# Group-norm statistics of batch entries 1 to 3 taken beside blocks of the first layer, and two steps of key preparation in a slot while an attention waits

## The chip, the cores and the metric

The kernel runs on one core of one Trainium2 chip. The metric is the device time of one execution in microseconds (us). Of a kernel several executions are timed and the median is taken; in addition one execution is recorded by the hardware profiler, and all durations below come from that one. Engines are named as in the profile: PE is the matrix engine (PEld its weight loads), DVE the vector engine, ACT the engine for activation functions, POOL the general one, and SP the engine from whose queue the transfers (DMAs) are issued.

## The reference, cut to what matters

The input `x` has 4 batch entries of 32 x 96 tokens (3072 tokens) with 256 channels, all in float32. Two layers are computed, each adding to `x`.

```python
def _gn(v, G=32, eps=1e-5):              # group norm: mean and variance per entry and
    g = v.reshape(B_, H_, W_, G, C_ // G)  # group of 8 channels, over all 3072 tokens
    m = jnp.mean(g, axis=(1, 2, 4), keepdims=True)
    s = jnp.var(g, axis=(1, 2, 4), keepdims=True)
    return ((g - m) / jnp.sqrt(s + eps)).reshape(v.shape)

# layer 0: a Mamba block along one image axis ("t"), then another along the other ("d")
x = x + _L0_conv_ref(_gn(x), ...)
# layer 1: additive attention within an entry, then a graph-gated mixture of 4 experts
t = _to_tokens(x)
t = t + _L1_attn_ref(_ln_t(t), ...)      # h = tanh(q_i + k_j + b); e = h . wa; softmax over j
t = t + _L1_ffn_ref(_ln_t(t), ...)
```

A Mamba block projects in, convolves over 4 steps, computes a decay and an input for each of 512 channels x 16 states, scans along time, sums over the states, gates and projects out. The attention needs a tanh for every pair of tokens and 32 hidden units: 4 x 3072 x 3072 x 32 of them. The group norm needs the statistics of the whole entry before the first token of that entry can be normalized. Each attention needs the keys and queries of all 3072 tokens of its entry, and these need the finished first layer of that entry.

## The kernel before, in words

**First layer.** `Layer0.run` (L551) walks through 64 blocks of 384 tokens. In the listing order they are: for entry 0 the eight "t" blocks, then block 0 of the "t" blocks of entry 1, then the eight "d" blocks of entry 0; for entry 1 the remaining seven "t" blocks, the first "t" block of entry 2, the eight "d" blocks of entry 1; and so on. So blocks 0 to 16 end entry 0, blocks 17 to 32 end entry 1, 33 to 48 entry 2, 49 to 63 entry 3. Blocks 0 to 16 are called `lead`: no attention runs beside them, and some of their work is put on other engines (sums over states by PE, some element-wise work on ACT) than in the later blocks. Block *n* is worked through in 48 slots; in them its scans and outputs (`back`, L353) are done, together with the projection and convolution of block *n + 1* (`front`, L172) and the last sums of block *n - 1* (`end`, L508). Each slot has two halves: the functions of `jobs[0]` (the scans, L402, and the decays dA on ACT, L385), then everything else (the inputs dB, L393, the front, the end). dB and the scans use tiles `bB` and `bC` that are loaded two ahead on the SP queue, 384 KB each. A block has 32 dB instructions, two in every three slots. They serve below as a clock of the slots.

**The order of work.** PE, ACT, DVE and POOL get their instructions in exactly the order in which these Python functions are called; only the DMA issues on SP are ordered by a scheduler. DVE, ACT and POOL work through their lists in that order, so an instruction that has to wait holds up everything behind it on its engine.

**Group norm before.** `group_norm` (L99) runs once, ahead of everything, for all four entries: for each entry and each half *k* of the channels it loads two pieces of 768 KB (two buffers of the tag "dt"), takes six `bn_stats` of 512 tokens (L120) and one aggregate; then a small matmul averages over the groups of 8 channels, three small DVE operations and a second matmul give the variance, and ACT takes the square root (L131). One reciprocal for all entries ends it (L132).

**Attention.** `whole` (L1949) steps the first layer alone until block 17 has reached slot 11, where entry 0 is known to be stored; then `Attention.units` (L778) and the first layer advance together, half a slot of each in turn. With one tanh of 128 x 3072 per slot (L815), an entry takes 768 slots. The scores of a tanh are computed two slots later by 16 small matmuls (L788), and after every eighth tanh there are softmax and value steps. Work that is less urgent (`side`: key preparation, and `after`, which prepares the second half of layer 1) is advanced by `beside()`, one step at a time, in slots where the attention has nothing else to do.

**Keys.** `keys(b)` (L720) yields 48 steps. The first 12 take layer-norm statistics of 256 tokens each (tile `x`, 256 KB, two buffers, L690; `bn_stats` L707 and aggregate L708). Then 12 times three steps follow: normalize two tiles (L703); transpose them on PE (L717) and copy the result out of PSUM (`xTc`, L718); multiply with both weights on PE (`pq`, L748) and copy into `qsel` (four small copies, L752) and `krep` (L755). Transposes and products share one PSUM buffer. Only when the 48 steps are done can the first tanh of that entry be issued. While `units` finds no `krep` for the next entry, it takes the branch at L803: no tanh, and one `beside()` per slot:

```python
            if b < B and "krep" not in self.state[b]:
                yield                      # first half of a slot of layer 0
                ...                        # late copies
                yield                      # second half
                beside()
                continue
```

**The end.** After block 63 no first layer is left; the rest of the attention runs beside a sort of the graph's edges (DVE), gathers (POOL) and early experts (PE, `early`). Then follows a tail with gathers, gates and the remaining experts.

Of the kernel before, what the change touches and what calls it, by code (L numbers as in the profile page):

```python
# [17 lines left out]
F32 = mybir.dt.float32  # L18
# [8 lines left out]
P = 128  # L27
B, NV, S, C = 4, 32, 96, 256
TOK = NV * S
# [45 lines left out]
class Layer0:  # L75
# [8 lines left out]
    def __init__(self, ctx, tc, ident, a, x1):  # L84
        self.nc = nc = tc.nc
        self.ident, self.a, self.x1 = ident, a, x1
        pool = lambda name, bufs, **k: ctx.enter_context(tc.tile_pool(name=name, bufs=bufs, **k))
        self.const, self.wk, self.st = pool("l0c", 1), pool("l0w", 1), pool("l0s", 2)
        self.ps, self.ps_u = pool("l0p", 1, space=PSUM), pool("l0u", 1, space=PSUM)
        self.dram = pool("l0d", 1, space=bass.MemoryType.DRAM)  # L90
        self.ps_x = pool("l0x", 1, space=PSUM)
        ps_a = pool("l0a", 1, space=PSUM)
        self.dA = [ps_a.tile([P, 512], F32, tag=f"dA{i}", name=f"dA{i}") for i in range(DA_BUFS)]
        self.turn, self.beside = 0, None
        self.xt = [self.dram.tile([KC, P, NV, S], F32, tag="xt", name="xt", bufs=3)
                   for _ in range(B)]
        self.group_norm()

    def group_norm(self):  # L99

        nc, wk, ps, const = self.nc, self.wk, self.ps, self.const
        gavg = const.tile([P, P], F32, tag="gavg", name="gavg")
        nc.sync.dma_start(gavg, self.a["gavg"])
        eps = const.tile([P, 1], F32, tag="eps", name="eps")
        nc.vector.memset(eps, 1e-5)
        self.gm = const.tile([P, KC, B], F32, tag="gm", name="gm")
        self.gr = const.tile([P, KC, B], F32, tag="gr", name="gr")
        HB = TOK // 2
        NB = HB // 512
        for b in range(B):  # L110
            gm = self.gm[:, :, b]
            mv = wk.tile([P, KC, 2], F32, tag="gmv", name="gmv")
            gv = wk.tile([P, KC], F32, tag="gv", name="gv")
            for k in range(KC):
                stats = wk.tile([P, 2, NB, 6], F32, tag="gst", name="gst")
                for i in range(2):
                    xs = wk.tile([P, HB], F32, tag="dt", name="xs", bufs=2)
                    nc.sync.dma_start(xs, self.a["xT"][k * P:(k + 1) * P, b, i * HB:(i + 1) * HB])
                    for j in range(NB):
                        nc.vector.bn_stats(stats[:, i, j, :], xs[:, j * 512:(j + 1) * 512])  # L120
                nc.vector.bn_aggr(mv[:, k, :], stats.rearrange("p i n s -> p (i n s)"))
            pg = ps.tile([P, T], F32, tag="pp", name="pg")
            nc.tensor.matmul(pg[:, :KC], gavg, mv[:, :, 0], start=True, stop=True)
            nc.vector.tensor_copy(gm, pg[:, :KC])

            nc.vector.tensor_tensor(gv, mv[:, :, 0], gm, ALU.subtract)
            nc.vector.tensor_tensor(gv, gv, gv, ALU.mult)
            nc.vector.tensor_tensor(gv, gv, mv[:, :, 1], ALU.add)
            pg2 = ps.tile([P, T], F32, tag="pp", name="pg2")
            nc.tensor.matmul(pg2[:, :KC], gavg, gv, start=True, stop=True)  # L130
            nc.scalar.activation(self.gr[:, :, b], pg2[:, :KC], AF.Sqrt, bias=eps)  # L131
        nc.vector.reciprocal(self.gr, self.gr)  # L132

    def weights(self, way, keys, bufs=1):

# [416 lines left out]
    def run(self):  # L552

        order, NBLK = [], TOK // T
        for b in range(B):
            order += [(b, "t", i) for i in range(1 if b else 0, NBLK)]
            if b + 1 < B:
                order.append((b + 1, "t", 0))  # L560
            order += [(b, "d", i) for i in range(NBLK)]
        blocks = [{"b": b, "way": w, "i": i, "L": S if w == "t" else NV, "lead": n <= 2 * NBLK}
                  for n, (b, w, i) in enumerate(order)]

        FRONT, STATES = ("in_x", "conv", "convb", "xproj", "dt", "dtb"), ("A", "D", "in_z")

        def states_weights(blk):
            blk["w"] = {**self.weights(blk["way"], ("A", "D"), 2), **self.weights(blk["way"], ("in_z",))}
            self.scale_states(blk["w"])

        first = blocks[0]
        self.wf = self.weights(first["way"], FRONT)
        self.scale_front(self.wf)
        states_weights(first)

        def alone(*parts):
            for slot in range(48):
                fs = [f for part in parts for f in part.get(slot, [])]
                for f in fs:
                    f()  # L580
                if fs:
                    yield None
                    yield None

        yield from alone(self.front(first, True))
        left, ending = ({}, {}), {}
        for n, blk in enumerate(blocks):
            then = blocks[n + 1] if n + 1 < len(blocks) else None
            old = blocks[n - 1] if n else None

            fresh = then and n + 2 < len(blocks) and blocks[n + 2]["way"] != then["way"]
            if old is None or old["way"] != blk["way"]:
                for t in self.dA:
                    self.nc.vector.memset(
                        t[:, :T].rearrange("p (q l) -> p q l", l=blk["L"])[:, :, 0:1], 0.0)
            for j in range(2):
                for name in ("bB", "bC"):
                    if not left[1]:
                        self.broadcast(blk, name, j)

            breaks = then and (then["way"], then["i"]) == ("d", 0) and then["b"] == blk["b"]
            jobs, later = self.back(blk, None if breaks else then)
            ahead = self.front(then, blk["lead"]) if then and not breaks else {}
            for slot in range(48):
                for f in left[0].get(slot, []) + jobs[0].get(slot, []):
                    f()
                yield None
                for part in (left[1], jobs[1], ending, ahead):
                    for f in part.get(slot, []):
                        f()  # L610
                if slot == 12:
                    if old is None or old["way"] != blk["way"]:
                        blk["wo"] = self.weights(blk["way"], ("out",))
# [24 lines left out]


class Attention:  # L640
# [135 lines left out]
    def units(self, side):  # L776
# [24 lines left out]
        while i < B * PER + LAG or todo or self.later:  # L801
            b, col = self.entry, self.col = divmod(i, PER)
            if b < B and "krep" not in self.state[b]:  # L803

                yield
                late, self.later = self.later, []
                for f in late:
                    f()
                yield
                beside()  # L810
                continue
# [433 lines left out]
class Graph:  # L1245
# [864 lines left out]
```

## Time and profile before

| What | us |
|---|---|
| Median of three executions (lowest, highest) | 15310.87 (15308.61, 15326.58) |
| The profiled execution, its own time | 15328.57 |
| Its span, first to last instruction | 15326.8 |
| PE, DVE, ACT, POOL busy in it | 11744.9, 11006.6, 12153.9, 8997.6 |

The span and the time of the profiled execution differ by 1.8 us, so sums over the span stand directly for time; that execution lies 17.7 us above the median. A row of instruction groups gives source line, engine, operation, output<-input with shapes and count; then the total busy time and the mean duration in ns; then the engine's idle time just before them and what ended it. "Granted clock" is the share of full speed that PE was given. A row of a table of stretches gives, behind the stretch and its length, the busy time and number of instructions of each engine, then the granted clock, the mean busy share of the 16 DMA engines and their GB/s.

### The profile page before, as it was taken

To read this page: it belongs to the slowest core of one execution; us is meant where nothing else is said; L and a number is where in the kernel's file an instruction comes from. 1 tells how busy PE (TensorE), PEld (TensorE's weight loads), DVE (VectorE), ACT (ScalarE), POOL (GpSimd) and SP (SyncE) were. 2 spreads that over 40 slices of the span, in tenths; PEclk is the share of its full clock that TensorE was granted. 3 is DMA by queue.
4 is the path that set the end of the run, shared out by engine and by line. 5 is a ranking of instruction groups with operands and counts; after the bars stand their busy time and mean duration, and the time that the engine had idled before them with its cause. 6 is when DMAs were issued, how large, how long until landed. Compare 5 with 4: busy or idle time off the path is not lost. (4 is left out here: it accounts for less than half of the span.)

```text
span 15326.8 us, 225317 instructions
## 1 busy us (share of the span) xinstructions
PE 11744.9 (77%) x86496; PEld 5137.0 (34%) x86496; DVE 11006.6 (72%) x15895; ACT 12153.9 (79%) x9327; POOL 8997.6 (59%) x6935
## 2 busy tenths in 40 slices
PE   5666764777777767788887777888876778988997
PEld 2222332222222233333333333333332334433554
DVE  7888888777777887777777877577778864321367
ACT  3443334999999979999999899999997889999221
POOL 4555556777777767767767677477750024400684
PEclk8888887888888888989998889999988989999998
DMA  5666665445445444454454444355531000010234
GB/s 192 204 203 200 198 204 167 149 148 156 152 150 151 158 156 148 150 152 151 151 150 156 147 149 152 110 156 151 154 127 37 24 13 13 10 31 22 66 95 138
DMA packets 1209121, 2007.93 MB, mean 131 GB/s; under 512 B 412384, under 2 KB 655712, under 8 KB 1204960
## 3 DMA queue, kind: packets, MB, share of 16 engines
q1 hardware_dynamic: 1180384, 1988.07, 41.6%
q0 software_dynamic: 27648, 5.36, 0.8%
q8 instruction: 680, 11.14, 0.3%
q14 instruction: 409, 3.35, 0.1%
HBM read 1875.19 MB, written 117.83 MB: 130 GB/s over the span
## 5 line engine op out<-in xcount | busy, mean ns | idle before, releaser
L815 ACT ACTIVATE th<-krep,qsel 128x3072 f32<-128x3072 f32 x3072 | 8661.7, 2848 | 411.1 <-PE pe L788 392.0
L788 PE MATMUL pe<-th,wa_blk 128*32 128x384 f32 x49152 | 4999.3, 535 | 1196.7 <-ACT pr L884 957.3
L409 POOL TENSOR_TENSOR h<-h,bC 128x768 f32<-128x768 f32 x2048 | 3756.2, 1834 | 3000.4 <-DVE h L402 2634.4
L402 DVE TENSOR_TENSOR_SCAN h<-dA,dB 128x384 f32<-128x384 f32 x4096 | 3687.3, 942 | 1109.4 <-ACT dA L385 752.9
L788 PEld LDWEIGHTS pe<-th,wa_blk 128*32 128x32 f32 x49152 | 1448.0, 116 | 3775.6 <-issue 1992.1
L393 DVE TENSOR_TENSOR dB<-bB,dtu 128x768 f32<-128x768 f32 x2048 | 1942.3, 948 | 123.3 <-DMA bB<-bc 91.2
L385 ACT ACTIVATE dA<-dt,t_A 128x380 f32<-128x380 f32 x2048 | 1127.1, 571 | 887.6 <-DVE h L402 883.1
L385 ACT ACTIVATE dA<-dt,d_A 128x372 f32<-128x372 f32 x2048 | 1102.9, 562 | 601.3 <-DVE h L402 595.9
L428 PE MATMUL py<-h,ident 128*128 128x384 f32 x2176 | 1010.1, 597 | 679.6 <-POOL h L409 678.2
L416 POOL TENSOR_TENSOR h<-h 128x768 f32<-128x768 f32 x752 | 1423.0, 1892 | 53.6
L900 PE MATMUL pv<-xn,pT 128*32 128x257 f32 x18432 | 1116.1, 391 | 172.3 <-DVE pT L893 171.4
L959 POOL TENSOR_SCALAR sf<-sel,f 128x32 f32<-128x32 f32 x384 | 148.6, 410 | 1641.6 <-ACT f L955 1533.9
L893 DVE COPY pT<-ptw 128x512 f32<-128x512 f32 (+1 forms) x768 | 419.0, 546 | 703.7 <-PE ptw L891 703.0
L428 PEld LDWEIGHTS py<-h,ident 128*128 128x128 f32 x2176 | 445.4, 223 | 1247.6 <-POOL h L409 1015.2
L900 PEld LDWEIGHTS pv<-xn,pT 128*32 128x32 f32 x18432 | 583.5, 112 | 759.7 <-DVE pT L893 317.4
L417 POOL TENSOR_TENSOR h<-h 128x384 f32<-128x384 f32 x752 | 783.7, 1042 | 59.0
L418 POOL TENSOR_TENSOR y<-y,h 128x384 f32<-128x384 f32 x752 | 779.9, 1037 | 59.0
L1714 ACT ACTIVATE h<-ph,b 128x512 f32<-128x512 f32 x148 | 96.7, 685 | 662.9 <-POOL pace L1047 473.9
L1337 POOL DMA_INDIRECT gs<-tab_s,si x432 | 526.6, 1219 | 131.3 <-issue 98.8
L891 PE MATMUL ptw<-ident,pr 128*128 128x128 f32 x2304 | 484.7, 328 | 143.5 <-DVE pT L893 79.6
L902 DVE COPY pvs<-pv 128x257 f32<-128x257 f32 x384 | 160.2, 417 | 569.0 <-PE pv L900 568.8
L1052 POOL DMA_INDIRECT gd<-tab_a,di x432 | 467.2, 1082 | 140.6 <-issue 133.4
(302 smaller groups left out, 15311.0 us busy)
## 6 DMA issues: line engine op xcount, KB each, us to landing
bB<-bc SPq DMA_DIRECT2D x2048, 384.0 KB
bC<-bc SPq DMA_DIRECT2D x2048, 384.0 KB
all<-kept SPq DMA_DIRECT2D x24, 2048.0 KB
x<-x SPq DMA_DIRECT2D x144, 256.0 KB
kept<-ko SPq DMA_DIRECT2D x59, 512.0 KB
x<-x SPq DMA_DIRECT2D x192, 128.0 KB
xt<-xn2T SPq DMA_DIRECT2D x41, 512.0 KB
qsel<-xn2T SPq DMA_DIRECT2D x75, 256.0 KB
```

Of the source, the lines that this page charges most:

```text
L385: nc.scalar.activation(inner(dA[:, :T]), inner(blk["dt"][:, e, :]), AF.Exp, scale=blk["w"]["A"][:, e, i + s:i + s + 1])
L393: nc.vector.tensor_tensor(dB, blk["bB"].pop(j), z["dtu"].unsqueeze(1).to_broadcast([P, SB, T]), ALU.mult)
L402: nc.vector.tensor_tensor_scan(h[:, s, :], z.pop(("dA", e, i + s))[:, :T], z["dB"][:, s, :], 0.0, ALU.mult, ALU.add)
L409: nc.gpsimd.tensor_tensor(h, h, blk["bC"].pop(j), ALU.mult)
L416: nc.gpsimd.tensor_tensor(h0, h0, h1, ALU.add)
L417: nc.gpsimd.tensor_tensor(h0[:, 0, :], h0[:, 0, :], h0[:, 1, :], ALU.add)
L418: nc.gpsimd.tensor_tensor(y[e], y[e], h0[:, 0, :], ALU.add)
L428: nc.tensor.matmul(z["py"], self.ident, h[:, s, :], start=(i == 0), stop=(i == DS - 1))
L788: nc.tensor.matmul(pe[q * QU:(q + 1) * QU, j, :KQ // 2], self.wa[:, k, :], th[:, c0:c0 + KQ // 2], start=(k == 0), stop=(k == NK - 1))
L815: nc.scalar.activation(th, s["krep"], AF.Tanh, bias=s["qsel"][:, col:col + 1])
L900: nc.tensor.matmul(pv[q * QU:(q + 1) * QU, :C + 1], pT[:, i, q * QU:(q + 1) * QU], s["xn"][:, q * NK + i, :], start=(i == 0), stop=(i == N ...
L1337: nc.gpsimd.indirect_dma_start(out=gs[:, u, :], out_offset=None, in_=rows, in_offset=bass.IndirectOffsetOnAxis(ap=ed.si[:, q, c0 + u:c0 + ...
```

## The change

Two things are changed.

1. `group_norm(b)` now does one entry at a time and only entry 0 ahead of the blocks. For entries 1 to 3 the work is cut into nine pieces, (entry, channel half 0), (entry, channel half 1), (entry, factors), and one piece is done beside each of the blocks 1, 2, 3 (entry 1), 17, 18, 19 (entry 2) and 20, 21, 22 (entry 3). A channel piece loads 1.5 MB in slot 0, and does its six `bn_stats` in slots 10, 12, 14, 17, 20 and 23; the factors are done in slots 0, 1 and 12. The tile `xs` now has the tag "uab", a single buffer of 128 x 3072 that `front` also takes in slot 32 of every block, and that a block's last additions read until slot 46. The reciprocal is taken per entry.
2. In the branch of `units` that waits for keys there is a second `beside()`, between the two halves of the slot.

```diff
-        self.group_norm()
+        self.norm_constants()
+        self.group_norm(0)
+        self.norms = [(b, k) for b in range(1, B) for k in range(KC + 1)]
...
+    def channel_norm(self, b, k):
+        def load():
+            v["x"] = self.wide("xs")
+            v["st"] = self.wk.tile([P, NB, 6], F32, tag="gst", name="gst")
+            for h in range(2):
+                cols = slice(h * TOK // 2, (h + 1) * TOK // 2)
+                nc.sync.dma_start(v["x"][:, cols], self.a["xT"][k * P:(k + 1) * P, b, cols])
+        def some(j):
+            nc.vector.bn_stats(v["st"][:, j, :], v["x"][:, j * 512:(j + 1) * 512])
+            if j == NB - 1:
+                nc.vector.bn_aggr(self.gmv[:, k, :], v["st"].rearrange("p n s -> p (n s)"))
+        return [load] + [lambda j=j: some(j) for j in range(NB)]
...
+    def factors(self, b):
+        def mean():        # matmul with gavg
+        def variance():    # copy, subtract, multiply, add on DVE
+        def mean2():       # second matmul with gavg
+        def root():
+            gr = self.gr[:, :, b]
+            nc.scalar.activation(gr, v["pg"][:, :KC], AF.Sqrt, bias=self.geps)
+            nc.vector.reciprocal(gr, gr)
+        return [mean, variance, mean2, root]
+
+    def norm_beside(self):
+        if not self.norms:
+            return {}
+        b, k = self.norms.pop(0)
+        if k == KC:
+            mean, variance, mean2, root = self.factors(b)
+            return {0: [mean], 1: [variance], 12: [mean2, root]}
+        return {slot: [f] for slot, f in zip((0, 10, 12, 14, 17, 20, 23), self.channel_norm(b, k))}
...
+            norms = self.norm_beside() if n in (1, 2, 3) or n > 2 * NBLK else {}
             for slot in range(48):
                 for f in left[0].get(slot, []) + jobs[0].get(slot, []):
                     f()
                 yield None
-                for part in (left[1], jobs[1], ending, ahead):
+                for part in (left[1], jobs[1], ending, ahead, norms):
                     for f in part.get(slot, []):
                         f()
...
             if b < B and "krep" not in self.state[b]:
                 yield
                 late, self.later = self.later, []
                 for f in late:
                     f()
+                beside()
                 yield
                 beside()
                 continue
```

More of the change, by code (lines that the diff above doesn't have):

```diff
@@ L96, in __init__ @@
                    for _ in range(B)]
-        self.group_norm()
[L99 to L105, printed above, removed]
+        self.norm_constants()
+        self.group_norm(0)
+        self.norms = [(b, k) for b in range(1, B) for k in range(KC + 1)]
@@ L106, in group_norm, with norm_constants @@
+    def norm_constants(self):
+        nc, const = self.nc, self.const
+        self.gavg = const.tile([P, P], F32, tag="gavg", name="gavg")
+        nc.sync.dma_start(self.gavg, self.a["gavg"])
+        self.geps = const.tile([P, 1], F32, tag="eps", name="eps")
+        nc.vector.memset(self.geps, 1e-5)
         self.gm = const.tile([P, KC, B], F32, tag="gm", name="gm")
         self.gr = const.tile([P, KC, B], F32, tag="gr", name="gr")
[L108 to L124, printed above, removed]
@@ new lines, in norm_constants, with group_norm @@
+        self.gmv = const.tile([P, KC, 2], F32, tag="gmv", name="gmv")
+    def group_norm(self, b):
+        for k in range(KC):
+            for f in self.channel_norm(b, k):
+                f()
+        for f in self.factors(b):
+            f()
+    def channel_norm(self, b, k):
+        nc = self.nc
+        NB = TOK // 512
+        v = {}
+        def load():
[9 more added lines that the diff above has]
+        return [load] + [lambda j=j: some(j) for j in range(NB)]
@@ L126, in group_norm @@
+    def factors(self, b):
+        nc, ps, mv, gm = self.nc, self.ps, self.gmv, self.gm[:, :, b]
+        v = {}
+        def mean():
+            v["pg"] = ps.tile([P, T], F32, tag="pp", name="pg")
+            nc.tensor.matmul(v["pg"][:, :KC], self.gavg, mv[:, :, 0], start=True, stop=True)
+        def variance():
+            nc.vector.tensor_copy(gm, v["pg"][:, :KC])
+            gv = v["gv"] = self.wk.tile([P, KC], F32, tag="gv", name="gv")
             nc.vector.tensor_tensor(gv, mv[:, :, 0], gm, ALU.subtract)
@@ L128, in group_norm @@
             nc.vector.tensor_tensor(gv, gv, mv[:, :, 1], ALU.add)
[L129 to L132, printed above, removed]
+        def mean2():
+            v["pg"] = ps.tile([P, T], F32, tag="pp", name="pg2")
+            nc.tensor.matmul(v["pg"][:, :KC], self.gavg, v["gv"], start=True, stop=True)
+        def root():
[11 more added lines that the diff above has]
+        return {slot: [f] for slot, f in zip((0, 10, 12, 14, 17, 20, 23), self.channel_norm(b, k))}
     def weights(self, way, keys, bufs=1):
```

## The prediction

> **What bounds the kernel now.** I read the page first: no engine is above 79% of the span, so the stages decide. Then a table of stretches, with one row per stage that the change touches. Behind the length stand the busy us and counts of PE, PEld, DVE, ACT and POOL, the granted PE clock, DMA share and GB/s.
>
> ```profile
> core 0: us, PE busy (x) PEld busy (x) DVE busy (x) ACT busy (x) POOL busy (x), PEclk, DMA share, GB/s
> 231.00:487.00 256.00, 160.42 (x385) 72.96 (x385) 223.30 (x264) 107.05 (x188) 152.15 (x96) 0.90 0.62 203
> 2354.60:2558.60 204.00, 86.22 (x200) 48.25 (x200) 169.82 (x288) 49.65 (x82) 134.53 (x92) 0.62 0.58 179
> 2713.00:2893.00 180.00, 131.41 (x1179) 50.82 (x1174) 141.21 (x187) 178.53 (x136) 137.75 (x101) 0.87 0.51 150
> 5489.00:5568.60 79.60, 42.14 (x100) 26.28 (x100) 71.63 (x113) 20.76 (x34) 52.33 (x36) 0.67 0.49 155
> ```
>
> Row one is two blocks of the first layer alone: DVE is busy 87%. Row two is the wait for the keys of entry 0 (block 17 slot 11 to block 18 slot 11, 32 dB instructions, so 48 slots): 4.25 us a slot, longer than the 3.75 us of row three, a block of 48 slots with a tanh in each, where ACT is busy 99%. Row four is the wait of entry 1, 19 slots at 4.19 us. So a waiting slot isn't idle time. The groups of DVE in row two say what fills it:
>
> ```profile
> L402 DVE TENSOR_TENSOR_SCAN h<-dA,dB 128x384 f32<-128x384 f32 x64 | 57.3, 936 | 0.1
> ...
> L703 DVE TENSOR_SCALAR x<-x,mv,lrs 128x256 f32<-128x256 f32 x24 | 16.3, 718 | 0.0
> L707 DVE BATCH_NORM_STATS2 lst<-x 128x6 f32<-128x256 f32 x24 | 9.8, 407 | 10.2 <-DMA x<-x 10.2
> L752 DVE COPY qsel<-pq 32x64 f32<-32x64 f32 x44 | 9.7, 220 | 16.3 <-PE pq L748 15.9
> L718 DVE COPY xTc<-pt 128x512 f32<-128x512 f32 x11 | 7.5, 686 | 2.5 <-PE pt L717 2.5
> ```
>
> The scans never wait (0.1 us): DVE is the bound, and all its idle time but some 5 us lies in front of key steps. The timeline shows one such wait:
>
> ```profile
> 2434.99 0.69 DVE L718 COPY xTc<-pt 128x512 f32<-128x512 f32 x1
> 2435.60 1.79 DVE L402 TENSOR_TENSOR_SCAN h<-dA,dB 128x384 f32<-128x384 f32 x2
> ...
> 2437.61 1.91 PE L748 MATMUL pq<-xTc,wx_rep 128*128 128x256 f32 x4
> ...
> 2439.56 0.92 DVE L752 COPY qsel<-pq 32x64 f32<-32x64 f32 x4 [2.17 <-PE pq L748]
> ```
>
> From the end of xTc to that of the product 3.8 us pass; the scans cover 1.7, DVE stands for the rest. Over the twelve tiles nine take 3.5 to 5.3 us and three 2.05: PE is slow here. Last, the start, and ACT while the attention runs (one row of a both-running block, one of the last stage):
>
> ```profile
> L120 DVE BATCH_NORM_STATS2 gst<-xs 128x6 f32<-128x512 f32 x48 | 30.1, 682 | 19.9 <-DMA xs<-in_xT 19.9
> ```
> ```profile
> 61.98 0.86 DVE L206 TENSOR_SCALAR xin<-xin,gm,gr 128x384 f32<-128x384 f32 x2
> ```
> ```profile
> L815 ACT ACTIVATE th<-krep,qsel 128x3072 f32<-128x3072 f32 x49 | 138.8, 2850 | 0.7 <-PE pe L788 0.6
> ```
> ```profile
> L815 ACT ACTIVATE th<-krep,qsel x213: 2835/2843/2879, 13497.4 to 14149.7; 128x3072 f32<-128x3072 f32 x107
> ```
>
> The norm holds back the first block until 61.98 us. In the last stage a tanh comes every 3.05 us (650 us by 213).
>
> **What the Trainium skill says.** "TensorE: Matmul & The Clock Gate", Part 1: the matrix clock is halved when PE hasn't been busy and comes back with activity. The trace agrees: 0.62 granted in the wait, 0.87 in the block, and products of 3.8 or 2.05 us. "Perfetto Trace Analysis", Tensor Engine Instruction: DVE and ACT are strict FIFO; so a key step that waits stops the scans behind it, as in the timeline. "ScalarE: Activation LUTs", Table sets: a switch of set costs 1283 ns of load plus about 1380 ns of drain; the trace has loads of 1.28 us (the drain it doesn't show apart).
>
> **Part 1, the norm.** *Removed from the start.* Entry 0 stays. Its first half of channels is aggregated at 10.22 us, as now. With a single buffer the next 1.5 MB are only issued then; the present loads took 4.4 us from issue (7.97) to use (12.34), and 768 KB more at the present 290 GB/s 2.6 us. So the last bn_stats end near 19 us, the aggregate (0.32) and the factors (17.84 to 20.2 in the trace, 2.4 us) near 21.7, then as now 60.2 to 61.98: the first xin at 23.5 to 25 us. I take 24: **-38** (-35 to -39; weights of 1.8 MB have to land as well).
> *Added beside blocks 1 to 3.* DVE: 2 x (6 x 0.682 + 0.32) = 8.8 us and about 1 for the factors, on the engine that bounds these blocks: +9 (a gain is excluded; +4 if half falls into DVE's waits). Two bursts of 1.5 MB stand in the SP queue among bB and bC, 5 us of transfer each at 290 GB/s; bB is loaded two ahead, 8 us at 2.7 us a slot, and DVE waits for it now about 5 us a block: +3 (0 to 8). The root needs two table loads (2.6 us) on an ACT that is 42% busy, behind which decays stand: +2.
> *Block 17.* The bn_stats in slots 12 to 23 fall into the wait, where DVE is the bound: +4.
> *Blocks 18 to 22.* DVE has 39 us of gaps in such a block, which cover most of 3 x 4.4 us: +3 (0 to 8). Two roots with two table loads and a wait for PE on an ACT without gaps: 2 x 3.5 = +7. The dA decays and the next tanh are queued behind them.
> Sum of part 1: -38 + 9 + 3 + 2 + 4 + 3 + 7 = **-10** (-20 to +3).
>
> **Part 2, the key steps.** *Slots.* Stepping through the loops of `run` and `units` gives the waits 48, 19, 0, 0 slots before and 24, 15, 10, 0 after. The second one shrinks little because entry 0's tanh now ends 24 slots earlier: only 24 slots remain in which key steps run beside a tanh, 18 of 48 are done there instead of 29, and 30 remain. For entry 2 a new wait of 10 slots appears (28 done beside tanh). Waiting slots fall from 67 to 49; slots after the last block fall from 860 to 842. Sort and early experts keep 658 and 761 slots, so no beside work falls into the tail.
> *Price of a step.* In row two the keys keep DVE 53 us busy (16.3 + 9.8 + 9.7 + 7.5 + 5.3 + 4.4) and 29 idle. That leaves 204 - 82 = 122 us for the first layer, 2.54 us a slot (POOL's 134.5 us set a floor of 2.8 that both versions exceed). A statistics step costs (14.2 + 10.2) / 12 = 2.0; a tile of three later steps (38.8 + 18.8) / 11 = 5.24, of which 1.5 is the wait for pq.
> *Two steps in a slot.* The work per step stays, but now half a slot of first layer lies between two steps: scans of 1.75 us or, in every third case, some 0.8 us of front. A pq of 3.8 us leaves 2.1 or 3.0, mean 2.5 instead of 1.5; with 0.2 for the transposes +1.2 a tile. No run shows this, so bounds: -0.5 (PE gets its full clock, 2.05 us) to +2.3 (4.6 us, matmuls of the front ahead, as in 2 of 12 tiles). Tile loads have half the time: +6 (-4 to +18).
> *Wait 0:* 24 x 2.54 + 24 + 6 + 12 x (5.24 + 1.2) = 168; then 24 slots with tanh at 3.75 = 90. Together 258 for 204: +54.
> *Wait 1:* the 67 slots from request to first tanh took 285.4 (205.8 with 29 steps beside tanh: (205.8 - 180) / 29 = 0.89 a step; 79.6 waiting). After: 52 x 3.75 + 18 x 0.89 + 15 x 2.54 + 10 x 6.44 = 313: +28.
> *Wait 2:* 305.9 for 67 slots with 48 steps: 3.93 a slot without them. After: 57 x 3.93 + 28 x 0.89 + 10 x 2.54 + 6.7 x 6.44 = 317: +11.
> *The end:* 18 slots fewer at 3.05: -55 (-51 to -63). If ACT weren't the bound there, this would be less.
> Sum of part 2: 54 + 28 + 11 - 55 = **+38**. The point is that a second key step costs a DVE-bound slot its full price, while beside a tanh it cost 0.89 us.
>
> **Together** +28: 15326.8 becomes about 15355 in span. The median lies 17.7 below the profiled execution; the difference moves it from 15310.9 to about 15339. A change of 0.2%, some 31 us, is about what a measurement of this kernel can tell from none; the forecast lies just inside, so "same" and "slower" share it.
>
> **Rivals.** *Cheap steps (faster).* Denser key work keeps PE's clock up. Per tile -0.5 instead of +1.2 on 28.7 tiles gives -49; with loads that keep pace and half of DVE's norm work in gaps -14: 28 - 63 = -35, **15276**. It decides from a pq below 2.5 us on. For it: the three tiles at 2.05 us. Against it: even with the tanh-free PE at 86 of 204 us the clock stayed at 0.62, and it is the chain DVE-PE-DVE, not PE, that sets the pace.
> *Late tiles (slower).* The first twelve steps load 256 KB each within six slots, beside 3 MB of xn and bB/bC; this stretch already runs at 80% DMA share with three stalls of 2.8 to 4.4 us. With +18 there and pq behind front matmuls (+2.3): 28 + 12 + 32 = +72, **15383**. For it: 10.2 us of such idle time at half the rate. Against: later tiles have 1.5 slots each.
> *The norm's transfers don't hide.* `xs` waits for uab on SP with bB and bC behind it; if each of six bursts stalls DVE 5 us: +27, **15366**. Against: uab is free from slot 46 on.
>
> **Chances.** Forecast 0.55 (15310 to 15370), cheap steps 0.15, late tiles 0.2, transfers 0.1. Faster by over 0.2%: 0.11, two thirds of the first rival. Same: half of the forecast, the rest of that rival and a little of the others, 0.38. Slower: 0.51. The range 15285 to 15395 leaves out the far end of the first rival and what exceeds +84, the sum of nearly all upper ends.
>
> **What would show it.** First xin near 24 us; the first tanh near 2508 (2565 - 38 + 14 + 4 - 36); waits of about 168 + 4, 102 and 68 us; idle time in front of L752, now 69.4 us for all entries, near 100; the last tanh to the end unchanged. The forecast is wrong if the waits get shorter than 150, 90 and 58, or if DVE stands in front of L707 for over 20 us.

## The result, and the profile after

| | before | after |
|---|---|---|
| Median of 7 executions each (us) | 15323.71 (15308.61 to 15326.75) | 15366.61 (15354.46 to 15381.13) |
| Profiled execution, its span (us) | 15328.57, 15326.8 | 15354.46, 15352.7 |

The changed kernel is slower: 1.0033 times the time before, with an interval of 1.0023 to 1.0042. That is 43 us by the medians, and 35 to 64 us by the interval. The two profiled executions differ by only 25.9 us, because that of after is its fastest and that of before lies 5 us above its median. Everything below that is read from a trace explains the 25.9; how the remaining 17 us are spread the traces don't show.

The table of stretches, for the kernel after. Its columns are those of the table before. The rows are two blocks of the first layer alone; the wait of entry 0; the 24 slots behind it, in which its first tanh run; a block with a tanh in each slot; the wait of entry 1; and the new wait of entry 2.

```profile
core 0: us, PE busy (x) PEld busy (x) DVE busy (x) ACT busy (x) POOL busy (x), PEclk, DMA share, GB/s
194.00:458.00 264.00, 171.47 (x388) 77.80 (x386) 232.30 (x280) 107.73 (x189) 152.80 (x97) 0.86 0.63 208
2323.90:2470.40 146.50, 63.01 (x166) 38.08 (x166) 105.72 (x221) 24.60 (x42) 65.85 (x45) 0.65 0.52 161
2470.40:2575.70 105.30, 67.42 (x502) 26.52 (x502) 88.53 (x115) 86.71 (x64) 67.27 (x48) 0.74 0.44 139
2758.90:2939.80 180.90, 131.75 (x1189) 50.70 (x1193) 137.84 (x186) 179.15 (x136) 135.40 (x100) 0.87 0.51 157
5423.40:5525.60 102.20, 53.42 (x140) 31.88 (x138) 77.49 (x132) 21.67 (x30) 47.38 (x34) 0.60 0.36 114
8610.30:8682.60 72.30, 40.50 (x121) 25.67 (x121) 46.33 (x84) 12.45 (x18) 32.15 (x22) 0.69 0.37 122
```

A waiting slot now takes 6.1 us (146.5 by 24), 6.8 (102.2 by 15) and 6.6 (72.3 by 11: the last row runs from slot 1 to slot 12, one slot more than the wait has), where it took 4.25 and 4.19. In the block in which the attention runs nothing differs: 180.9 us for 180.0, and ACT full in it.

The groups of DVE in the wait of entry 0, after:

```profile
L444 DVE TENSOR_TENSOR_SCAN h<-dA,dB 128x384 f32<-128x384 f32 x33 | 29.6, 937 | 0.0
...
L747 DVE TENSOR_SCALAR x<-x,mv,lrs 128x256 f32<-128x256 f32 x22 | 12.5, 609 | 1.4 <-DMA x<-x 1.4
L751 DVE BATCH_NORM_STATS2 lst<-x 128x6 f32<-128x256 f32 x24 | 9.8, 407 | 14.2 <-DMA x<-x 14.2
L796 DVE COPY qsel<-pq 32x64 f32<-32x64 f32 x44 | 9.7, 220 | 21.0 <-PE pq L792 20.6
L762 DVE COPY xTc<-pt 128x512 f32<-128x512 f32 x11 | 7.4, 673 | 0.0
```

In half the slots DVE stands longer for the tiles (14.2 us for 10.2) and for the products (21.0 for 16.3), and no longer for the transposes (0.0 for 2.5). One such tile in the timeline, after: start, duration, engine, and in brackets the idle time before:

```profile
2431.14 0.68 DVE L762 COPY xTc<-pt 128x512 f32<-128x512 f32 x1
2431.74 1.79 DVE L444 TENSOR_TENSOR_SCAN h<-dA,dB 128x384 f32<-128x384 f32 x2
...
2433.74 1.91 PE L792 MATMUL pq<-xTc,wx_rep 128*128 128x256 f32 x4
...
2435.69 0.44 DVE L796 COPY qsel<-pq 32x64 f32<-32x64 f32 x2 [2.16 <-PE pq L792]
```

From the end of xTc (2431.82) to that of the product (2435.65) 3.8 us pass, as before; two scans cover 1.7, and DVE stands for 2.16. How long a product takes goes with the clock. Two rows in the columns of the table of stretches, one for this product and one for a product of 2.05 us in the same wait:

```profile
2431.87:2435.65 3.78, 3.78 (x9) 3.07 (x10) 1.66 (x2) 1.16 (x2) 1.80 (x1) 0.50 0.30 92
2404.75:2406.75 2.00, 1.96 (x8) 1.40 (x8) 1.93 (x4) 0.00 (x0) 1.92 (x2) 1.00 0.30 104
```

PE was granted half of its clock (0.50) in the one and all of it (1.00) in the other. Of the eleven products in this wait six had 0.50 throughout and took 3.8 us, three had 1.00 and took 2.05, and two lie between (3.42 and 3.49). Last the start (the groups of the first 30 us, and a line of the timeline) and the tanh of the last stage:

```profile
L133 DVE BATCH_NORM_STATS2 gst<-xs 128x6 f32<-128x512 f32 x12 | 7.5, 682 | 9.9 <-DMA xs<-in_xT 9.7
```
```profile
23.04 0.87 DVE L248 TENSOR_SCALAR xin<-xin,gm,gr 128x384 f32<-128x384 f32 x2
```
```profile
L860 ACT ACTIVATE th<-krep,qsel x212: 2833/2843/2880, 13497.8 to 14149.4; 128x3072 f32<-128x3072 f32 x106
```

12 bn_stats stand ahead of the first block instead of 48, the first xin comes at 23.04 us instead of 61.98, and a tanh of the last stage still takes 3.07 us.

To see where the 25.9 us went, both executions are cut at the same blocks and slots, found by counting the dB instructions (block.slot):

| Stretch | before | after | difference | forecast |
|---|---|---|---|---|
| start to 0.0 | 105.7 | 69.2 | -36.5 | -38 |
| to 4.0 (norm of entry 1) | 509.7 | 520.1 | +10.4 | +14 |
| to 17.11 | 1739.2 | 1734.6 | -4.6 | 0 |
| to 19.11 (wait of entry 0 and its first tanh) | 395.2 | 435.0 | +39.8 | +58 |
| to 24.0 (norm of entries 2 and 3) | 867.3 | 882.4 | +15.1 | +10 |
| to 33.11 | 1666.0 | 1680.6 | +14.6 | 0 |
| to 36.0 (wait of entry 1) | 561.0 | 588.1 | +27.1 | +28 |
| to 49.0 | 2522.9 | 2492.9 | -30.0 | 0 |
| to 52.0 (wait of entry 2) | 620.8 | 618.0 | -2.8 | +11 |
| to 63.46 | 2388.6 | 2424.6 | +36.0 | 0 |
| to the last tanh | 2825.1 | 2783.4 | -41.7 | -55 |
| to the end | 1125.1 | 1123.8 | -1.3 | 0 |

Two things stand out. The waits cost what was forecast or less, and three stretches in which the change puts no work of its own moved by -30 to +36 us. The stretches for which the forecast had a number sum to +11 us, those that it put at 0 to +15.

### The profile page after: what moved, and what is told of

Its sections match the earlier page's. It is cut to its first block, busy times and chain, and to the rows that moved or that the text cites. A ratio compares the mean times of both kernels' runs of the same rounds, so it can differ in the third digit from the quotient of the medians.

```text
span 15352.7 us, 225436 instructions
## 1 busy us (share of the span) xinstructions
PE 11794.1 (77%) x86496; PEld 5160.4 (34%) x86496; DVE 11028.0 (72%) x15898; ACT 12161.8 (79%) x9333; POOL 8990.6 (59%) x6935
## 4 chain that ended last, share of the span: by engine, by line
PE 17%; ACT 16%; DVE 9%; issue 4%; POOL 4%; DMA 1%; DVEq 0%; SPq 0%; POOLq 0%; ACTq 0%
ACT th L860 11%; PE pe L832 7%; PE pv L945 3%; ACT dA L427 2%; POOL gs L1382 2%; DVE h L444 1%; PE po L1685 1%; PE pa L1433 1%; PE ptw L936 1%; DVE go L1135 1%; PE ph L1677 1%; ACT pr L929 1%; PE ex L1591 1%; POOL gd L1097 1%; DVE dB L435 1%
## 5 line engine op out<-in xcount | busy, mean ns | idle before, releaser
L936 PE MATMUL ptw<-ident,pr 128*128 128x128 f32 x2304 | 496.3, 335 | 156.6 <-DVE pT L938 105.3
L1382 POOL DMA_INDIRECT gs<-tab_s,si x432 | 531.2, 1230 | 131.3 <-issue 98.9
L922 DVE TENSOR_REDUCE nb<-pe 128x1 f32<-128x768 f32 x384 | 362.5, 944 | 279.1 <-PE pe L832 279.0
```

What stands on the lines that cost most here:

```text
L1382: nc.gpsimd.indirect_dma_start(out=gs[:, u, :], out_offset=None, in_=rows, in_offset=bass.IndirectOffsetOnAxis(ap=ed.si[:, q, c0 + u:c0 + ...
```

## The experiments

All kernels here compute the whole result. Each is compared with executions of the kernel before on the same chip (49, 44 or 8 of them, with medians of 15327.18, 15322.09 and 15316.17). My theory was that of the prediction: part 1 gains a little, part 2 loses more, since a second key step in a slot costs DVE its full price and the wait for its product. The rivals: part 1's transfers cost more than thought; and the loss comes from somewhere else than the key steps.

**Each part alone.** `norm_only` is the kernel after without the second `beside()`:

```diff
                 for f in late:
                     f()
-                beside()
                 yield
                 beside()
                 continue
```

> Part 1 alone, one key step per waiting slot. Forecast of the prediction: -10 us against before (-20 to +3): first xin 38 us earlier, +14 in blocks 1 to 3, +4 in the wait of block 17, +10 in blocks 18 to 22. Rival (the norm's transfers and its work on a bound DVE eat more than the start gives): +10 to +30 us. The waits for keys stay at 204 + 4 and 79.6 us.

Measured: 15306.06, ratio 0.9987 (0.9981 to 0.9994), so about -20 us. Its stretches: start -36.6, blocks 0 to 3 +8.6, block 17 slot 11 to block 19 slot 11 +1.8, then +4.3 to block 24. The statistics in block 17 cost almost nothing, because they stand where DVE would otherwise stand for tiles. In front of the statistics of the keys it stood 10.2 us before, and in `norm_only`:

```profile
L751 DVE BATCH_NORM_STATS2 lst<-x 128x6 f32<-128x256 f32 x24 | 9.7, 405 | 5.7 <-DMA x<-x 5.6
```

`steps_only` is the kernel before with that one line added.

> Part 2 alone, group norm ahead of everything as before. Forecast of the prediction: +38 us against before (waits 168, 102, 68 us, 55 us back at the end). From the whole change, measured +43, less part 1 at -10: about +53. Rival (part 1 is what made the change slower): -20 to +10 us. If the time lies between 30 and 60 the second key step is the cause.

Measured: 15383.53, ratio 1.0043 (1.0029 to 1.0057), so +66 us. Part 2 is the loss, and the rival of part 1's transfers falls: that part gains on its own, and -20 + 66 gives the measured +43 within 3 us. Its stretches, cut as in the table above: +41 and +25 us for the waits of entries 0 and 1 with what follows them, +9 and +15 in the two stretches between them, -24 in blocks 36 to 48, +46 in blocks 52 to 63, and -42 at the end. So the waits less the end, which is what the prediction counted, are +24 of the 66; the rest lies in stretches without key steps.

**What a key step costs in a slot.** `steps_held` is `steps_only` with the first tanh of entries 0 and 1 held back to the slots they have in the kernel before, so that the end and all later slots stay as they were:

```diff
-            if b < B and "krep" not in self.state[b]:
+            if b < B and ("krep" not in self.state[b]
+                          or self.waited[b] < {0: 48, 1: 19}.get(b, 0)):
+                self.waited[b] += 1
```

> Part 2 alone, but the first tanh of entries 0 and 1 is held back until as many slots have passed as before (48 and 19): two key steps per slot, then slots with neither key step nor tanh, and everything later in the slots of the kernel before. Theory (a second step costs a slot its full price, and an empty slot is bound by POOL at 2.8 us): 148 + 67 = 215 us for 204, and 68 + 25 = 93 for 80; all later stretches within 8 us of before; total +20 to +30 us. Rival (an empty slot saves what a double slot costs, because each tile's chain is as long as ever): total within 8 us of before.

Measured: 15351.07, ratio 1.0019 (1.0011 to 1.0027), +29 us. Its table of stretches; the rows are the 24 slots with two steps, and the 24 that follow with neither key steps nor tanh:

```profile
2346.40:2493.10 146.70, 65.24 (x166) 39.46 (x166) 100.88 (x212) 24.60 (x42) 65.89 (x45) 0.63 0.51 160
2493.10:2570.20 77.10, 29.18 (x46) 12.62 (x46) 63.99 (x83) 25.24 (x40) 66.31 (x46) 0.55 0.51 165
```

Here is the price list that the forecast lacked. By these rows a slot without a key step takes 3.21 us (77.1 by 24, with POOL busy 86% of it), one with a step 4.25 (204 by 48, before), one with two 6.11. The rows are cut about a slot ahead of the first step, so the steps of the last tile, 6.8 us of DVE's time, still fall into the second. An estimate in which each row begins with one to one and a half slots of the kind that stand ahead of it gives 3.0 to 3.1, 4.3 and 6.2 to 6.3 us: the first step of a slot costs 1.2 to 1.3 us, the second about 2.0. DVE's work grows nearly evenly (2.67, 3.54 and 4.20 us a slot by the rows), its idle time doesn't: 0.55, 0.71 and 1.91 us. So the waits of a single step mostly fall into time in which DVE would stand anyway, and most of those of the second are paid.

The two sums came to 223.8 and 97.0 us, above the 215 and 93 expected, as an empty slot takes more than 2.8 us. From block 17 slot 11 to block 19 slot 11, where the key steps are over in both kernels, the same steps in the same slots cost 14.3 us more in pairs, and from block 33 slot 11 to block 36 another 13.3. That is 28 us, for +29 by the medians. All other later stretches stay within 4 us of those before. Ahead of the change, in blocks 4 to 17, the two executions differ by 9.3 us although the kernels are alike there: so much one stretch can move by itself.

**Is it the wait for the product?** `after_reordered` normalizes the next tile between the transposes and the products of a tile, so that DVE has more to do while PE works. The steps are the same:

```diff
-        for j in range(N):
-            ahead = self.tiles_of(x1, j + 1) if j + 1 < N else None
-            ...  # normalize x, tile j
-            yield
-            xT = self.transposed(x)
-            x = ahead
-            yield
+        ahead = self.tiles_of(x1, 1)
+        ...  # normalize x, tile 0
+        yield
+        for j in range(N):
+            xT = self.transposed(x)
+            x, ahead = ahead, self.tiles_of(x1, j + 2) if j + 2 < N else None
+            yield
+            if j + 1 < N:
+                ...  # normalize x, tile j + 1
+                yield
             pq = self.psum("pq")
```

> The changed kernel with the three steps of a tile in another order: the next tile is normalized between the transposes and the products of a tile, so the product pq has two half slots and 1.4 us of normalizing to cover it. Same steps, same slots, same work. Theory (DVE stands for pq, 21 + 20 + 24 us of idle time before the qsel copies in the three waits of the changed kernel): that idle time falls below 10 us in all, waits of about 127, 84 and 52 us, and the time falls by 50 to 70 us, to about 15,305, below the kernel before. Rival (the waiting slot is full of DVE's own work, and the idle time only moves to other instructions): less than 20 us gained, waits within 8 us of 146, 102 and 72.

Measured: 15323.15, ratio 1.0000 (0.9991 to 1.0008), some 43 us below the kernel after, a little less than expected. The waits went to 142.8, 79.5 and 56.2 us from 146.5, 102.2 and 72.3. In the second, where DVE had stood 19.7 us in front of the qsel copies and now stands 3.9, the wait for the product was most of what was saved. In the first nearly nothing was, as the rival has it; the groups of DVE there, of this kernel:

```profile
L747 DVE TENSOR_SCALAR x<-x,mv,lrs 128x256 f32<-128x256 f32 x24 | 27.5, 1187 | 1.5 <-DMA x<-x 1.5
...
L800 DVE COPY qsel<-pq 32x64 f32<-32x64 f32 x44 | 9.6, 219 | 3.4 <-PE pq L796 2.9
```

DVE stands 3.4 us for the products instead of 21.0, but the normalizations take 27.5 us instead of 12.5 (24 of them in this stretch, 22 there). They now run while POOL is busy. In the wait of the kernel after, 14 of 22 ran with POOL idle and took 0.41 us each, and 8 beside it, 0.96. In this one 2 ran alone (0.41), 6 began just before a POOL instruction (0.39), and 16 began while one ran. Of these 15 ended 0.15 us after that POOL instruction did, whatever was left of it, and took 1.07 to 1.96 us. A pair of normalizations in the timeline:

```profile
2387.33 2.21 DVE L747 TENSOR_SCALAR x<-x,mv,lrs 128x256 f32<-128x256 f32 x2
2387.49 1.89 POOL L451 TENSOR_TENSOR h<-h,bC 128x768 f32<-128x768 f32 x1 [5.33 <-DVE h L444]
```

The first of the two was under way when POOL began, and took 0.39 us; the second ended just behind POOL. The Trainium skill, "SBUF — State Buffer", Who interferes with whom, says that VectorE and GpSimd share a pair of ports under an exclusive lock: an operation of VectorE that uses two port pairs, and it counts `tensor_scalar` among those that can, is held until the other's instruction ends. The trace agrees with that in time; no run shows the ports themselves.

So the next kernel, `after_act`, takes the normalization of waiting slots (`self.waiting`) off DVE, to ACT, which was busy only 24.6 of 146.5 us there in the kernel after:

```diff
+        nm = self.rows.tile([P, NT], F32, tag="lnm", name="lnm")
+        nc.vector.scalar_tensor_tensor(nm, mv[:, :, 0], -1.0, rs, ALU.mult, ALU.mult)
...
-                self.normalized(x[:, i, :], x[:, i, :], mv, rs, n)
+                if self.waiting:
+                    nc.scalar.activation(x[:, i, :], x[:, i, :], AF.Identity,
+                                         bias=nm[:, n:n + 1], scale=rs[:, n:n + 1])
+                else:
+                    self.normalized(x[:, i, :], x[:, i, :], mv, rs, n)
```

> The reordered kernel, and while an attention waits the two normalizations of a tile are done by ACT (Identity with a scale and an added constant per row) instead of DVE; ACT is busy about a fifth of that time. In the reordered kernel DVE no longer stood for pq in the first wait (3.4 us of idle time instead of 21.0), yet that wait stayed at 143 us: the 24 normalizations grew from 12.5 to 27.5 us. They take 0.41 us where POOL is idle and up to 1.9 us where a POOL instruction runs. Theory (a normalization is held until the POOL instruction beside it is over, so moved into the gaps of pq it only waits for POOL): without it on DVE the waits are 115 to 125, 62 to 70 and 45 to 52 us (reordered: 143, 80, 56), the time 40 to 55 us below the reordered kernel, about 15,275. Rival (the wait moves on once more, to another DVE instruction or to POOL): waits within 8 us of the reordered kernel's.

Measured: 15300.42, ratio 0.9985 (0.9978 to 0.9992), -22 us against before and some 18 to 23 below `after_reordered`. The waits are 133.6, 76.6 and 53.2 us, all above what the theory said; the second and third shrank by 3 us, as the rival has it. In the first, 27.5 us of DVE work went and the wait shrank by 9. The groups say where the rest is:

```profile
L751 DVE BATCH_NORM_STATS2 lst<-x 128x6 f32<-128x256 f32 x24 | 9.8, 408 | 13.7 <-DMA x<-x 13.7
L810 DVE COPY qsel<-pq 32x64 f32<-32x64 f32 x40 | 8.8, 220 | 19.5 <-PE pq L806 19.1
```

The 16 us in front of the qsel copies came back. What is taken off DVE between a product's start and its end isn't gained here. That fits a chain DVE, PE, DVE that sets the pace of paired steps, with DVE's own work only filling it; no run changes the length of the product alone to show it.

**The stretches that nothing touches.** As 48 slots are six times eight, an attention's units of eight tanh begin at the same slots modulo 8 in every block of an entry. That remainder is set by the slot of the entry's first tanh. It is 3, 6, 6 for entries 0, 1, 2 before, and 3, 2, 4 after. If it decides, moving a start alone moves these stretches. `before_phase` is the kernel before with the first tanh of entry 1 held four slots more (`{1: 23}` in the condition shown above), which makes it 3, 2, 2:

> The kernel before, with the first tanh of entry 1 held back by four slots more (23 waiting slots instead of 19), so that entry 1's units of eight tanh fall on the slots of the blocks as in the changed kernel (slot 34 modulo 8 is 2, as slot 2 there; before it was 30, so 6). Theory (how the units of eight fall on a block's slots is worth tens of us per entry, which explains 38 us less in blocks 36 to 48 of the changed kernel): blocks 36 to 48 take 25 to 40 us less than before, and the total is 10 to 35 us below before although four slots are added. Rival (that difference comes from elsewhere, or from one execution to the next): blocks 36 to 48 within 8 us of before, total +5 us (four slots at about 1 to 1.5 us).

Measured: 15295.4, ratio 0.9981 (0.9974 to 0.9988), -29 us, with four slots *more* of waiting. Blocks 36 to 48 take 2506.3 us for 2522.9, 17 us less where 25 to 40 were expected; with the stretches on either side (-5.9 and -3.6) that is 26 of the 29 us. `after_phase` is the kernel after with entry 2 held two slots more, which makes it 3, 2, 6:

> The changed kernel with the first tanh of entry 2 held back by two slots (12 waiting slots instead of 10), so that it starts in slot 14, which is 6 modulo 8 as slot 30 was before, instead of 12, which is 4. Theory (the place of the units of eight in a block's slots made blocks 52 to 63 take 2425 to 2438 us instead of 2388 to 2396): they take 2385 to 2400 us again and the time falls by 25 to 45 us to about 15,330. Rival (something else of the change slows these blocks): 2420 us or more there, and the time rises by 2 to 4 us.

Measured: 15329.81, ratio 1.0006 (0.9997 to 1.0015), so +8 against before, in an interval that takes in no change at all, where the kernel after has +43. Blocks 52 to 63 take 2404.7 us, just above what was expected: 20 of the 36 us came back. The stretches of all kernels, from one execution of each, by the remainder of the entry that runs in them:

| Stretch | remainder 6 | 2 | 4 |
|---|---|---|---|
| 36.0 to 49.0 (entry 1) | before 2522.9, norm_only 2519.6, steps_held 2523.3 | before_phase 2506.3, norm_phase 2492.8, norm_phase_act 2492.0, after 2492.9, after_phase 2493.2, steps_only 2498.5, after_reordered 2505.2, after_act 2499.8 | |
| 52.0 to 63.46 (entry 2) | before 2388.6, norm_only 2395.6, steps_held 2392.4, after_phase 2404.7 | before_phase 2387.8, norm_phase 2387.4, norm_phase_act 2379.8 | after 2424.6, steps_only 2434.9, after_reordered 2438.1, after_act 2425.0 |

In the first row all kernels with 6 lie above all with 2, by 24 us in the mean. In the second 4 stands 35 us above 6, and 2 some 10 below it, though those two groups all but touch. In that row what differs is how long ACT stands in front of a tanh for the scores that free its buffer. From the table of waits, ACT in the stretch from 52.0 to 63.46, before:

```profile
ACT th L815 <- PE pe L788: 62.3, 57, 3.9
```

after:

```profile
ACT th L860 <- PE pe L832: 94.8, 80, 4.4
```

and in `after_phase`:

```profile
ACT th L862 <- PE pe L833: 73.9, 55, 4.2
```

The columns are total us, times and the longest. Of the 36 us that this stretch is longer in the kernel after, 32.5 lie in this one wait. Which instructions of PE stand ahead of the scores at a bad remainder stays open.

**Putting it together.** `norm_phase` has part 1, single steps, and entry 1 held four slots.

> Part 1 alone with entry 1 held back four slots as in the kernel that only did that. If the two gains are independent they add: -20 and -31, about -50 us, 15,276. If the norm's gain depends on where the units fall: -25 to -40.

Measured: 15270.25, ratio 0.9967 (0.9955 to 0.998), -52 us: the gains of `norm_only` and `before_phase` add up. `norm_phase_act` adds the reordered keys and the normalization on ACT while waiting, still with one step in a slot:

> The kernel with part 1 alone and entry 1 held back, and with both changes of the keys (next tile normalized between transposes and products, and on ACT while an attention waits), still one key step per waiting slot. Theory (DVE is the bound of a waiting slot, and its time there goes to the first layer, to key work and to standing for pq and for POOL): without 16 us of normalizing and most of 19 us of standing the first wait falls from 202 to 165 to 178 us, the second to 60 to 70 at its 19th slot, the time by 35 to 55 us to about 15,225. Rival (with one step per slot the product is mostly covered already, and another wait takes its place): 0 to 20 us.

Measured: 15243.62, ratio 0.9954 (0.994 to 0.9968), -73 us, which is 21 to 27 below `norm_phase`, between what the theory and the rival said. The wait of entry 0 went from 202.2 to 180.1 us. The groups of DVE in it, in `norm_phase`:

```profile
L748 DVE TENSOR_SCALAR x<-x,mv,lrs 128x256 f32<-128x256 f32 x24 | 16.2, 716 | 0.0
...
L797 DVE COPY qsel<-pq 32x64 f32<-32x64 f32 x44 | 9.7, 220 | 17.1 <-PE pq L793 16.7
```

and in `norm_phase_act`, where the first of these rows is gone:

```profile
L811 DVE COPY qsel<-pq 32x64 f32<-32x64 f32 x44 | 9.6, 219 | 11.8 <-PE pq L807 11.4
```

Here, with one step in a slot, the 16.2 us taken off DVE are gained and the wait for the product falls by 5.3. Together that is nearly the whole gain of this wait. In the second wait nearly nothing was gained: its 19 slots take 78.7 us for 79.7. The copies behind the products there, in `norm_phase`, where normalizing took 10.7 us of DVE:

```profile
L797 DVE COPY qsel<-pq 32x64 f32<-32x64 f32 x24 | 5.3, 220 | 7.5 <-PE pq L793 7.2
```

and in `norm_phase_act`:

```profile
L811 DVE COPY qsel<-pq 32x64 f32<-32x64 f32 x28 | 6.2, 220 | 15.1 <-PE pq L807 14.8
```

DVE has less to do and stands for the products instead, 7.6 us longer (with one tile more among them), as in the pairs of `after_act`. Why a single step gains in one wait and not in the other stays open. ACT takes 0.59 us for each of these normalizations. This kernel is the fastest of the study.

## Why the forecast held, and where its steps were off

The median lies 28 us above the forecast of 15339, inside the range and just inside the likeliest case's own (15310 to 15370). Of these 28, 13 are the kernel before, for which the forecast took the 15310.9 us of three executions and seven give 15323.7; the change itself is +43 for +28. That part 1 gains and part 2 loses more is shown by `norm_only` and `steps_only`; that the second step of a slot is dearer than the first, by `steps_held`. That the sum came so near is partly luck. In the traces the terms of the forecast give +11 us instead of +28, and what it put at 0 gives +15. With 20 us of that taken back, in `after_phase`, the change costs +8 us, hardly to be told from nothing.

*Part 1* was forecast at -10 and measured -20. The start was right (first xin 23.04 us for 24). The work beside the blocks was priced too high: 8.6 for 14 us in blocks 1 to 3, and 1.8 + 4.3 for 14 us in blocks 17 to 22. The waits for tiles in block 17 cover the statistics there (5.7 us of standing for 10.2), which the step "DVE is the bound: +4" had left out. The roots brought the table loads that were counted, of 1.28 us each: 16 for 12 between block 19 slot 11 and block 24. (The price that the prediction quotes for them stands on the page it names under What ACT_TABLE_LOAD costs, not under Table sets.) The +15 of the whole change up to block 24 is near the +10 of the forecast by chance: 9 of it come with the key steps, as `steps_only` shows.

*The waits.* 146.5, 102.2 and, over eleven slots, 72.3 us for 172 (168 and 4), 102 and, over ten, 68. The first is the one mis-sized. The step "a pq of 3.8 us leaves 2.1 or 3.0, mean 2.5" had the pieces right (2.16 with two scans between, 3.5 with none), but three of the eleven products in the wait took 2.05 us, and the mean is 1.9 (21.0 by 11). With the transposes' 2.5 us gone, where more was expected, "+1.2 a tile" came out at +0.2 (4.7 less 2.5, by 11). Normalizing took some 3 us less, as more of it ran with POOL idle (14 of 22, for 9 of 24 before), and the late tiles cost 4 us for 6. The sum also holds all twelve tiles, while the steps of the last, 6.8 us of DVE's time, fall behind the 146.5 us. The part of the step that said 24 slots with tanh take 3.75 us each was too low: they took 105.3, 4.39 each. That price was of a block in full run; in the kernel before, too, the first 24 slots behind the wait took 98.9 us, 4.12 each, with the end of the last tile in them. Taken over both blocks the loss is 39.8 for 58. In front of the qsel copies of all entries DVE stands 109.7 us, where "near 100" was named (69.4 before).

*Wait 1* was right (+27.1 for +28), *wait 2* too high by the stretch (-2.8 for +11) though not by the waiting slots (6.6 us each for 6.8). *The end* gave 41.7 for 55. Up to the first tanh of entry 3 it gave 58.8 us; but the 768 tanh of that entry then took 17.1 us more, and for 14.6 of them ACT stood longer for the scores (125.7 us for 111.1). That work which stood beside the 18 slots now stands beside these tanh would explain it, but isn't shown.

*A term was missing:* the stretches given 0 in the table sum to +15 us in this trace (-4.6 + 14.6 - 30.0 + 36.0 - 1.3). The -4.6 is no more than one execution differs from another there. The -30 and +36 go with the remainders, as two starts that were moved alone show for 17 and 20 us. The +14.6 comes with the key steps (+14.5 in `steps_only`, -0.1 in `norm_only`). Two steps of preparation for layer 1 moved into it and seven into the stretch before it; at the 0.89 us of a step beside tanh that is an estimated 2 and 6 us, and the rest of the +14.6 stays open.

*The signs named.* First xin right; the first tanh at 2480.8 us and not near 2508, because of the shorter first wait; the waits not all above the bounds of 150, 90 and 58: the first, at 146.5, is just below, by the named test a sign against the theory. `steps_held` shows that it doesn't mean cheap steps: a double slot still costs some 2 us more than a single one. DVE stood 14.2 us in front of the statistics in that wait, under the 20 named. Last tanh to end 1123.8 for 1125.1: unchanged.

*The rivals.* Cheap steps (15276): no, although the clock did rise, 0.65 for 0.62. Late tiles (15383): no, 4 us more of standing for tiles in the first wait, not 18, and no product later than 3.84 us there. Transfers that don't hide (15366): the median meets this number, but not for this reason, since `norm_only` shows that part 1 gains twice what was forecast; what was missing and the higher median of the kernel before put it there.

## What to carry to other kernels

Work that is slipped under another stream can get dearer with each piece in a slot: the first key step cost an estimated 1.2 to 1.3 us, the second about 2.0, so packing it into half the slots lengthened the whole although it ended earlier. Before doubling, look for what the pieces share: here a product that mostly takes 3.8 us between two pieces of DVE's work, and that a single step has a slot's work to cover. And when a change shifts the start of a periodic stream against another, look at stretches that it doesn't touch. Here a start moved alone moved them by 17 and 20 us, and holding a start by two or four slots gained more (35 and 29 us in all) than part 1 did (20).

## What the runs showed of the hardware

- A normalization (DVE, 128x256 float32, 0.41 us alone) that begins while a POOL instruction runs is mostly held until that one is over. Over the whole kernel after, 104 ran with POOL idle and took 0.40 to 0.41 us; of 71 that began while POOL ran, 56 ended 0.15 to 0.16 us after its instruction, having taken up to 1.96 us, and 8 ended before it. Normalizing `xin` took 0.45 to 0.48 us when POOL was idle or began later, and 0.77 to 2.03 in the other 53 cases.
- Other operations of DVE in that kernel differ by where their inputs lie. The gate L293, with two inputs in SBUF, took 0.55 us with POOL idle and 1.15 in the mean where it began while POOL ran. dB and the scans, whose second input (`dtu`, `dA`) is a PSUM tile, took 0.94 to 0.95 us in the mean either way, and bn_stats of the keys, with one input, 0.41 to 0.42. The page named above says so too: two inputs in SBUF contend with a GpSimd instruction that reads SBUF, and at most one doesn't.
- The product of a key tile, eight matmuls, begun at once takes 3.8 us from the end of xTc at a granted clock of 0.50 and 2.05 us at 1.00. In the first wait of after three of eleven had the full clock, in the second none of nine, in the third two of seven, which PE began late (2.8 and 4.7 us).
- The effect of the remainder repeats: kernels with the same one agree within some 16 us in stretches of 2,380 to 2,520, whatever else was changed in them.
